# Four layers on one core: first images loaded ahead of the constants, one image held in a big tile, and new due times for the order of work

## The chip, the core and the metric

The kernel runs on one core of a Trainium2 chip. The core has five engines that run side by side: TensorE (PE, matrix products; its weight loads are listed apart as PEld), VectorE (DVE), ScalarE (ACT), GpSimd (POOL) and SyncE (SP), which here only issues DMA transfers. GpSimd issues some transfers too. All of them wait for each other through semaphores, and each engine executes its own instructions strictly in the order in which they stand in its program. The metric is the device time of one execution in microseconds (us); lower is better.

## The reference

The input is 16 images of 96 channels and 56 x 56 pixels (L = 3136). Four layers follow each other.

```
# layer 0: masked inverted bottleneck, 96 -> 576 -> 96
h = relu(bn(conv1x1(x, w_pw1))) * mask_dilate * vector
h = relu(bn(dwconv3x3(h))) * mask * vector
x = x + bn(conv1x1(h, w_pw2)) * mask

# layer 1: a four-direction selective scan (VMamba style) and an MLP
u = silu(dwconv3x3(layernorm(z) @ in_proj))          # 192 channels
dt, B, C = split(einsum(xs, x_proj))                 # four scan directions
dt = softplus(dt @ dt_proj + bias); a = exp(dt * A)
h[l] = a[l] * h[l-1] + dt * B * xs; y = h * C + D * xs
z = z + layernorm(sum of the four y) @ out_proj
z = z + gelu(layernorm(z) @ fc1) @ fc2; x = x + z

# layers 2 and 3, each: a Fourier filter and a quantized MLP
t = t + bn(ifft(relu(complex_scale(fft(relu(bn(ln(t) @ w1)))))) @ w2)
t = t + ffn(ln(t))      # inputs of the products rounded to fp8, sums to fp16
```

## The kernel before

The three functions `layer0`, `layer1` and `layers23` run one after the other, each with its own pools of on-chip memory. Layer 0 leaves its images in x1, layer 1 leaves its in x2, both in device memory. A layer can only start its loads once the memory that its tiles take over from the layer before is free.

**The order of the work.** Within a layer the instructions are not issued in source order. Each piece of work is a Python generator; before a group of instructions it yields an `Op` that names an engine, a guessed cost, buffers that it takes and gives back, and lists that it waits for. `in_order` (from line 277) keeps a clock for each engine and at each step picks, of all waiting pieces, the one with the smallest start plus `late`: `late(us, op)` (line 271) shifts the rank of one operation by a due time. A negative value lets it go ahead of others, a positive one lets others go ahead of it. Once picked, the instructions are recorded, so the order on every engine, on SP's DMA queue too, is fixed before the chip runs. The guessed costs decide nothing else, except one thing: `filling` (lines 348 to 358) puts filler products of the identity with itself on PE (line 354), in a number that follows from how long the planner sees PE idle:

```
for _ in range(min(int((idle[0] - 0.4) / 0.23), 32)):
    nc.tensor.matmul(p[:, :P], ident, ident, start=True, stop=True)
```

They fill the PE's idle time, and their results are overwritten. What stands in a layer's prologue (loads of constants, folding of weights) is recorded before `in_order` runs.

**Layer 1.** Per image there are these pieces. `front` loads the image in four pieces of up to 896 columns into "xc" (two buffers), squares each half on ACT into "xn" (one buffer, L761), sums both on PE (p_s, L767 and L768), copies the sums on DVE (L770) and takes the power -1/2 on GpSimd (L779). Then it loads the four pieces once more, spreads r over the channels by PE transposes (p_r, L789), multiplies on DVE into "xn" (L794), projects (p_in, L799), convolves by nine products per tap set (p_c, L840), applies SiLU, and makes the scan's inputs (p_x, L882), which go to device memory as bc (L895). `made_of` makes dt (p_d, L923, softplus L925) and a (exponential, L934), and loads the rows of bc as "rb" and "rc" (two buffers each, L945 and L949). `driven` multiplies dt on DVE by u (L978) and by rb (L982); `scanned` scans (L1002, L1004), multiplies by rc (L1009), adds into y (L1016, L1021), and at an image's end folds the two halves of ym (L1024). `back` does the rest for each group of 448 pixels: squares (L1049), p_o (L1056 to L1059), the power, p_y (L1079), z (L1082, L1084), sums and power again, p_t, p_f, GELU (L1117), p_g, and the store (L1128). The pieces of different images overlap. Seven big tiles of 128 x 3136 are handed around ("big"); the last of them also holds the raw constants during the prologue.

**Layers 2 and 3.** Four lanes hold one image each in a tile t. A lane is set to zero once by GpSimd (L1581, inside `lane`), then for each image t is loaded in two halves through SP (L1587), its mean and squares are reduced on DVE (L1318, L1313) and ACT (L1310), r is a power on GpSimd (L1330), and transposes (p_t, L1348), the projection p_a (L1358), and the short Fourier product (L1372) write to device memory (d, L1383), from where z is read back transposed (z<-d) for the next product (L1399). The lanes start 40 us apart in the planner's time.

Of the kernel before, what the change touches and what calls it, by code (L numbers as in the profile page):

```python
# [39 lines left out]
F32 = mybir.dt.float32  # L40
# [8 lines left out]
L = S * S  # L49
# [557 lines left out]
def layer1(ctx, tc, src, given, dst):  # L607
# [19 lines left out]

    ident = ph.c([P, P], "ident")
# [7 lines left out]
    big = [ph.c([P, L], f"big{i}") for i in range(buffers["big"])]  # L636
# [94 lines left out]
    def front(b, it):  # L731

        def loaded(g):
            n = min(896, L - 896 * g)
            x = buf([C, 896], "xc")[:, :n]
            nc.sync.dma_start(x, given[b][:, 896 * g : 896 * g + n])
            return x


        yield Op("POOL", 0.5, take=("x",))  # L740
# [5 lines left out]
        yield late(-1.0, Op("POOL", 0.7, take=("half",)))  # L746
# [8 lines left out]
        def sums(g):  # L755
            yield Op("SP", 0.3, 4.0, take=("xc",))
            x = loaded(g)
            for i in range(x.shape[1] // T):
                yield late(-0.2, act(T, take=("xn",)))
                sq = buf([C, 2, T], "xn")[:, 0]  # L760
                nc.scalar.activation(sq, x[:, T * i : T * i + T], AF.Square)  # L761
                last = i == x.shape[1] // T - 1
                yield late(0.2, pe(8, 0.193, give=("xn", "xc") if last else ("xn",)))
# [10 lines left out]
        yield late(-23.8, dve(0, over=0.4))  # L774
# [3 lines left out]
        yield late(1.6, Op("POOL", 6.5))  # L778
        nc.gpsimd.tensor_tensor(r, v, nhalf, ALU.pow)  # L779

        def projected(g):
            banks = 2 if g < 3 else 1
            yield late(0.2, Op("SP", 0.3, 4.0, take=("xc",)))
            x = loaded(g)
            yield late(-0.6, pe(4 * banks, 0.096, ("ps", "xn")))
# [6 lines left out]
            yield dve(448 * banks, give=("ps", "xc"))  # L792
            xn = buf([C, 2, T], "xn")[:, :banks]
            nc.vector.tensor_tensor(xn, x.rearrange("c (b n) -> c b n", n=T), p[:C, :banks, :T], ALU.mult)  # L794
            for j in range(2):
                yield pe(banks, 0.75, ("ps",), ("xn",) if j else ())
# [13 lines left out]
                for i, (low, row, n) in enumerate(parts):  # L810
# [3 lines left out]
                    yield act(S * n, over=0.15, give=("ps",) if i == len(parts) - 1 else ())  # L814
# [6 lines left out]
        yield [projected(g) for g in range(4)]  # L821
        it["u"] = us = []
        for j in range(2):
            yield late(0.4, Op("none", 0.0, 0.0, take=("big",)))
            us.append(big.pop(0))

        def convolved(j):

            pad, u = (whole, halves)[j], us[j]
            for c in range(0, (8, 4)[j], 2):  # L830
                yield Op("none", 0.0, 0.0, take=("ps",))
                p = pair("p_c")
                yield late(0.5, pe(9, 0.66, (), table="quarters"))
# [25 lines left out]
                for i, (out, in_, cost) in enumerate(outs):  # L859
                    yield late(0.4, act(cost, over=0.05, give=("ps",) if i == len(outs) - 1 else ()))  # L860
                    nc.scalar.copy(out, in_)
            yield late(-0.5, act(L, give=("x" if j == 0 else "half",), table="silu"))
# [7 lines left out]
        def inputs(g):  # L870
            yield late(1.0, pe(4, 1.42))
# [11 lines left out]
            yield late(-0.2, act(SUB, over=0.16, give=("ps",)))  # L883
# [7 lines left out]
        yield late(-52.7, Op("SP", 2.8, 4.0, post=it["ready"]))  # L891
# [13 lines left out]
    def made_of(it):  # L905
# [4 lines left out]
        def steps():  # L910

            for unit in units:
                i, h = unit
                order = (0, 1) if i < 3 else (1, 0)
                for s in order:
                    yield late(0.2, Op("none", 0.0, 0.0, take=("dt",)))
                    made[unit][s] = dt = buf([P, SUB], "dt")
                    yield late(-60.5, pe(1, 0.66, table="halves"))
# [5 lines left out]
                    yield late(-0.6, act(SUB, over=0.08, give=("ps",), table="softplus"))  # L924
# [4 lines left out]
                yield late(-39.2, Op("none", 0.0, 0.0, take=("a",)))  # L929
                made[unit]["a"] = a = buf([P, HALF], "a")  # L930
                for s in order:
                    give = ("proj",) if last and s == order[1] else ()
                    yield late(-0.6, act(SUB, over=0.18, give=give, table="exp", post=times[unit, s]))
                    nc.scalar.activation(a[:, SUB * s : SUB * s + SUB], made[unit][s], AF.Exp, scale=aneg[:, i : i + 1])  # L934

        def rows_of(k, tag):

            for unit in units:
                i, h = unit
                for s in halves_of(unit):  # L940
                    yield late(0.8, Op("SP", 0.2 if i in GROUP else 0.4, 4.0, take=(tag,), post=it[tag][unit, s]))
# [42 lines left out]
    def scanned(it):  # L984

        before, held = None, False
        for unit in units:
# [3 lines left out]
            if unit in ((0, 0), (2, 0)):  # L991
                yield Op("none", 0.0, 0.0, take=("big",))
                it["y"].append(big.pop(0))
            y = it["y"][mixed]
            for s in halves_of(unit):
                own, as_own, each = views(unit, s)
                yield late(-0.4, dve(SUB, 2.09e-3, wait=it["driven"][unit, s], give=("a",) if held else ()))
# [25 lines left out]
        yield late(-85.7, dve(L, 1.85e-3))  # L1023
        nc.vector.tensor_tensor(image(ym[:64]), image(ym[:64]), turned(ym[64:]), ALU.add)  # L1024

    def back(b, it):
# [4 lines left out]
        def group(g, own=None):  # L1031
# [15 lines left out]
            yield late(-0.3, act(T, take=tags("ysq")))  # L1047
            sq = new([P, 2, T], "ysq")
            nc.scalar.activation(sq[:, 0], y0[:, cols], AF.Square)  # L1049
            yield late(-28.8, act(T))  # L1050
# [15 lines left out]
            if it["left"] == 0:  # L1066
                big.extend((y0, ym))
                yield late(-11.7, Op("none", 0.0, 0.0, give=("big", "big")))
            small = lambda n: work.tile([Q, 4], F32, tag=n, name=n, bufs=8)
            v, r = small("v4"), small("r4")  # L1070
            yield late(-118.1, dve(0, over=0.33, give=("ps",)))
            nc.vector.scalar_tensor_tensor(v, o[:, :, C], -1.0, o[:, :, C], ALU.mult, ALU.mult)
            nc.vector.scalar_tensor_tensor(v, v, EPS, p[:Q, 4:, 0], ALU.add, ALU.add)
            yield Op("POOL", 1.85)
            nc.gpsimd.tensor_tensor(r, v, nhalf[:, :4], ALU.pow)
            yield late(-0.5, pe(4, 0.185, tags("ps", "z")))
# [6 lines left out]
            yield late(-31.0, dve(4 * C, give=("ps",)))  # L1083
# [3 lines left out]
            yield act(4 * C, take=tags("zn"))  # L1087
            zn = new([Q, 4, C], "zn")
            nc.scalar.activation(zn, z, AF.Square)
            yield late(-0.1, dve(4 * C))  # L1090
            nc.vector.tensor_reduce(s1, z, AX.X, ALU.add)
            yield late(-18.1, dve(4 * C, over=0.53))
# [4 lines left out]
            yield late(-45.2, Op("POOL", 1.85))  # L1097
# [3 lines left out]
            yield late(-19.7, pe(4, 0.085, tags("ps", "zt"), tags("zn")))  # L1101
# [3 lines left out]
            yield late(0.3, act(T, over=0.04, give=("ps",)))  # L1105
# [5 lines left out]
            yield late(-6.9, pe(3, 0.75, (), tags("zt")))  # L1111
# [3 lines left out]
            for j in range(3):  # L1115
                yield late(-0.7, act(T, over=0.16, table="gelu", give=("ps",) if j else (), lag=0.14 if j == 2 else 0.0))
                nc.scalar.activation(hid[:, j], ps[j // 2][:, j % 2, :T], AF.Gelu, bias=b_fc1[:, j : j + 1])  # L1117
            yield late(0.9, pe(16, 0.193, ("ps",), tags("hid", "xr")))
# [6 lines left out]
            yield dve(4 * C, give=("ps",))  # L1125
            nc.vector.tensor_tensor(z, z, p[:Q, :4, :C], ALU.add)
            yield late(-8.1, Op("SP", 0.3, 2.0))
# [34 lines left out]
    def makes():  # L1162
        for b in range(B):
            yield -1
            yield Op("none", 0.0, 0.0, wait=items[b]["ready"])
# [8 lines left out]
    def scans():  # L1174
        for b in range(B):
# [3 lines left out]
            yield late(2.0, Op("none", 0.0, 0.0, post=items[b]["done"]))  # L1179
# [457 lines left out]
```

## Time and profile before

| | us |
|---|---|
| Median of 3 runs (lowest, highest) | 7235.88 (7232.42, 7246.8) |
| The profiled execution | 7242.65 |
| Its span | 7240.9 |

| stretch of the span, us | what runs | PE busy | DVE busy | PE clock |
|---|---|---|---|---|
| 100 to 1640 | layer 0 | 1530.50 | 1493.40 | 1.00 |
| 1680 to 1720 | opening of layer 1 | 28.51 | 6.93 | 0.55 |
| 1760 to 1800 | first image's convolution | 39.76 | 0.00 | 1.00 |
| 2229 to 4480 | layer 1 in steady state | 2169.12 | 2081.45 | 0.99 |
| 4850 to 4890 | last groups of layer 1 | 28.38 | 3.87 | 0.92 |
| 4890 to 4950 | opening of layers 2 and 3 | 29.97 | 25.38 | 0.70 |
| 4950 to 5050 | their first transfers | 77.17 | 57.84 | 0.86 |
| 5600 to 7050 | layers 2 and 3 in steady state | 1378.82 | 1259.11 | 0.98 |

How to read the profile: a row of the windows view gives a stretch, its length, then the busy time of each engine with the number of instructions in brackets, the clock granted to PE as a share of full speed, the busy share of the 16 DMA engines, and what they moved in GB/s. A row of the groups view gives line, engine, operation, output<-inputs with shapes and count, then busy time and mean of one in ns, and, behind the last bar, the idle time of the engine just before these instructions with what ended it. A row of the timeline gives start, length, engine, line and, in square brackets, the idle time before it and its releaser. A matrix product of fp32 data shows as two records. The busy time of PE contains the fillers.

### The profile page before, as it was taken

What the parts mean: (1) busy time and instruction counts of PE and PEld (TensorE: products, weight loads), DVE (VectorE), ACT (ScalarE), POOL (GpSimd) and SP (SyncE); (2) the same over time, 40 slices, a digit from 0 to 9 for tenths busy, and PEclk for the clock granted to TensorE, in tenths of its full rate; (3) what the DMA queues carried; (4) which work ended last, traced back from release to release, by engine and by line L of the source; (5) the groups of instructions that cost most, each with busy time, mean ns of one, the idle gap of its engine ahead of it and who ended that gap; (6) DMA issues with size and microseconds to landing.
All of it is one profiled execution on the core that took longest, in us unless ns stands there. A gap on an engine that the chain in (4) does not pass through costs nothing.

```text
span 7240.9 us, 139640 instructions
## 1 busy us (share of the span) xinstructions
PE 6845.1 (95%) x57794; PEld 4734.2 (65%) x57794; DVE 6329.1 (87%) x8036; ACT 4814.4 (66%) x6165; POOL 1050.8 (15%) x804
## 2 busy tenths in 40 slices
PE   7999999999999999999999999986999999999998
PEld 3444444445666666666666666666887887887887
DVE  8999999992899999999999999965888898898897
ACT  4454544442677777777777777744777777777776
POOL 1000000000021222122222222121111111111111
PEclk9999999998999999999999999998999999999999
DMA  1100010001544444444444444426556656656653
GB/s 36 27 26 26 19 28 24 22 13 28 141 129 129 129 129 130 122 130 132 131 129 130 128 132 133 119 79 136 133 122 152 133 125 139 145 129 142 141 120 89
DMA packets 550245, 743.44 MB, mean 103 GB/s; under 512 B 258281, under 2 KB 388873, under 8 KB 546729
## 3 DMA queue, kind: packets, MB, share of 16 engines
q1 hardware_dynamic: 548425, 731.41, 40.3%
q8 instruction: 455, 7.45, 0.4%
q0 software_dynamic: 1184, 3.10, 0.2%
q14 instruction: 181, 1.48, 0.1%
HBM read 542.35 MB, written 191.99 MB: 101 GB/s over the span
## 4 chain that ended last, share of the span: by engine, by line
PE 39%; DVE 14%; ACT 10%; issue 4%; DMA 4%; SPq 1%; POOL 0%; ACTq 0%; DVEq 0%; POOLq 0%
PE p_c L840 6%; PE p L1399 4%; PE p_a L1358 4%; ACT y L1541 3%; PE p_x L882 2%; PE p_g L1123 2%; PE p_d L923 2%; PE p_g L1554 2%; PE p_v L1440 2%; PE p_v L1441 2%; PE p_u L1451 2%; PE p L1372 2%; DVE dt L1009 2%; DMA xc<-x 2%; DVE dt L982 2%
## 5 line engine op out<-in xcount | busy, mean ns | idle before, releaser
L558 DVE SCALAR_TENSOR_TENSOR h<-pad,l_dw,h 128x1568 f32<-128x1568 f32 x704 | 1260.8, 1843 | 2.5
L530 PE MATMUL p_c<-pad,taps 64*64 64x392 f32 x8064 | 685.6, 490 | 1.5 <-ACT h L546 0.8
L1330 POOL TENSOR_TENSOR r<-v,nhalf 120x16 f32<-120x16 f32 (+1 forms) x128 | 364.0, 2911 | 1913.2 <-DVE v L1328 1487.0
L978 DVE TENSOR_TENSOR dt<-dt,big 128x784 f32<-128x784 f32 x384 | 457.0, 1190 | 116.3 <-ACT a L934 114.0
L530 PEld LDWEIGHTS p_c<-pad,taps 64*64 64x64 f32 x8064 | 302.0, 132 | 363.5 <-issue 355.5
L546 ACT ACTIVATE h<-p_c,shift 128x392 f32<-128x392 f32 x336 | 226.4, 674 | 396.3 <-PE p_c L530 393.0
L925 ACT ACTIVATE dt<-p_d 128x784 f32<-128x784 f32 x384 | 315.6, 822 | 236.4 <-PE p_d L923 233.4
L503 PE MATMUL p<-x,l_w 96*128 96x448 f32 (+3 forms) x1280 | 428.3, 512 | 6.0 <-DVE y L595 3.2
L1399 PE MATMUL p<-k_f,z 112*128 112x112 f32 x3072 | 388.6, 286 | 26.3 <-DMA z<-d 20.4
L1399 PEld LDWEIGHTS p<-k_f,z 112*128 112x128 f32 x3072 | 371.6, 200 | 59.4 <-ACT y L1541 31.9
L509 ACT ACTIVATE pad<-p,bn_t,bn_s 128x896 f32<-128x896 f32 (+2 forms) x432 | 322.4, 800 | 122.8 <-PE p L503 120.5
L840 PE MATMUL p_c<-x,taps 64*64 64x392 f32 x4608 | 394.2, 491 | 0.0
L1440 PE MATMUL p_v<-w,gg 128*112 128x97 f32 x2048 | 374.4, 265 | 6.0 <-ACT o L1559 4.7
L982 DVE TENSOR_TENSOR dt<-dt,rb 128x784 f32<-128x784 f32 x384 | 371.0, 966 | 3.2 <-DMA rb<-bc 2.1
L1441 PE MATMUL p_v<-w2both,gg 128*112 128x97 f32 x2048 | 373.1, 264 | 0.0
L1009 DVE TENSOR_TENSOR dt<-a,rc 128x784 f32<-128x784 f32 x384 | 371.9, 969 | 0.7
L580 PE MATMUL p<-h,l_w 128*96 128x392 f32 x1024 | 362.1, 496 | 1.3 <-ACT h L561 0.9
L923 PE MATMUL p_d<-proj,l_dt 64*128 64x392 f32 x1536 | 363.0, 550 | 0.0
L934 ACT ACTIVATE a<-dt,aneg 128x784 f32<-128x784 f32 x384 | 343.4, 941 | 17.1 <-DVE a L1004 14.9
L1004 DVE TENSOR_TENSOR_SCAN a<-a,dt 128x784 f32<-128x784 f32 x192 | 351.5, 1831 | 1.1
L1002 DVE TENSOR_TENSOR_SCAN a<-a,dt 128x784 f32<-128x784 f32 x192 | 351.1, 1829 | 0.5
L503 PEld LDWEIGHTS p<-x,l_w 96*128 96x128 f32 (+1 forms) x1280 | 208.0, 180 | 217.2 <-issue 177.0
(336 smaller groups left out, 16966.9 us busy)
## 6 DMA issues: line engine op xcount, KB each, us to landing
rb<-bc SPq DMA_DIRECT2D x256, 392.0 KB
rc<-bc SPq DMA_DIRECT2D x256, 392.0 KB
d<-v SPq DMA_DIRECT2D x448, 192.0 KB
z<-d SPq DMA_DIRECT2D x128, 672.0 KB
rb<-bc SPq DMA_DIRECT2D x256, 196.0 KB
rc<-bc SPq DMA_DIRECT2D x256, 196.0 KB
d<-v SPq DMA_DIRECT2D x256, 169.8 KB
v<-d SPq DMA_DIRECT2D x192, 194.0 KB
```

What stands on the lines that cost most here:

```text
L503: nc.tensor.matmul(p[n * i : n * i + n, t, :size], w1[:, P * j : P * j + n], images[b]["x"][:, cols], start=True, stop=True,)
L530: nc.tensor.matmul(p[to : to + 64, t, :TC], taps[64 * s : 64 * s + 64, j, i], pad[64 * s : 64 * s + 64, r0 : r0 + 7, i % 3 : i % 3 + S], s ...
L558: nc.vector.scalar_tensor_tensor(out, view, dw[:, j, i : i + 1], out, ALU.mult, ALU.add)
L840: nc.tensor.matmul(p[to : to + 64, b, :TC], taps[64 * s : 64 * s + 64, j, k], pad[64 * s : 64 * s + 64, r0 : r0 + 7, k % 3 : k % 3 + S], s ...
L923: nc.tensor.matmul(p[:, b, :TC], wdt[on, i], proj[on, at : at + TC], start=True, stop=True)
L978: nc.vector.tensor_tensor(as_own(dt), as_own(dt), own(u), ALU.mult)
L982: nc.vector.tensor_tensor(dt, dt, made["rb", s], ALU.mult)
L1009: nc.vector.tensor_tensor(dt, a, made["rc", s], ALU.mult)
L1330: nc.gpsimd.tensor_tensor(r, v, nhalf[:, :n], ALU.pow)
L1399: nc.tensor.matmul(p[:, q, :Q], flat[:, P * (3 * q + k) : P * (3 * q + k) + P], f2, start=True, stop=True)
L1440: nc.tensor.matmul(out, gs[2 * h][:, at + k], w["w2"][:, 2 * h], start=True, stop=False)
L1441: nc.tensor.matmul(out, gs[1][:, at + k], w["w2both"][:, h], start=False, stop=True)
```

## The change

It has three parts; nothing of what is computed changes.

1. In layer 1 the first image is loaded ahead of the constants, half through SP and half through GpSimd's queue, into a big tile. `front` treats image 0 apart (`held`): it reads the image from this tile in both passes, and puts the squares and later the normalized pieces into a second big tile, so that neither "xc" nor "xn" is taken. Both tiles are given back after the projection.
2. In layers 2 and 3 the four tiles t are allocated and zeroed ahead of everything else, two on GpSimd and two on DVE, and the first two images are loaded ahead of the constants. The lanes no longer zero their tile, and do not load the first two images.
3. The due times (`late`) of some hundred yields in layers 1 to 3 are other numbers; some are dropped, some are new. Costs, buffers and instructions stay as they were.

```diff
@@ layer1
+    big = [ph.c([P, L], f"big{i}") for i in range(buffers["big"])]
+    for k, engine in enumerate((nc.sync, nc.gpsimd)):
+        cols = slice(L // 2 * k, L // 2 * k + L // 2)
+        engine.dma_start(big[0][:C, cols], given[0][:, cols])
     ident = ph.c([P, P], "ident")
...
-    big = [ph.c([P, L], f"big{i}") for i in range(buffers["big"])]
     stage, used = big[-1], 0
...
+        held = b == 0
+        tags = (lambda *t: ()) if held else lambda *t: t
+        yield late(-10.2, Op("none", 0.0, 0.0, take=("big", "big") if held else ()))
+        if held:
+            image_, mixed = big.pop(0), big.pop(0)
+
         def loaded(g):
             n = min(896, L - 896 * g)
+            if held:
+                return image_[:C, 896 * g : 896 * g + n]
...
-            yield Op("SP", 0.3, 4.0, take=("xc",))
+            yield late(-12.6, Op("SP", 0.0 if held else 0.3, 0.0 if held else 4.0, take=tags("xc")))
...
-                yield late(-0.2, act(T, take=("xn",)))
-                sq = buf([C, 2, T], "xn")[:, 0]
+                yield late(0.2, act(T, take=tags("xn")))
+                at = 896 * g + T * i
+                sq = mixed[:C, at : at + T] if held else buf([C, 2, T], "xn")[:, 0]
...
-            xn = buf([C, 2, T], "xn")[:, :banks]
+            if held:
+                xn = mixed[:C, 896 * g : 896 * g + T * banks].rearrange("c (b n) -> c b n", n=T)
+            else:
+                xn = buf([C, 2, T], "xn")[:, :banks]
...
         yield [projected(g) for g in range(4)]
+        yield Op("none", 0.0, 0.0, give=("big", "big") if held else ())
+        if held:
+            big.extend((image_, mixed))
...
-            yield late(1.0, pe(4, 1.42))
+            yield late(0.7, pe(4, 1.42))
             p = pair("p_x")
...
-                    yield late(0.2, Op("none", 0.0, 0.0, take=("dt",)))
+                    yield late(-36.2, Op("none", 0.0, 0.0, take=("dt",)))
                     made[unit][s] = dt = buf([P, SUB], "dt")
-                    yield late(-60.5, pe(1, 0.66, table="halves"))
+                    yield late(-161.2, pe(1, 0.66, table="halves"))
                     p = pair("p_d")
...
-                yield late(-39.2, Op("none", 0.0, 0.0, take=("a",)))
+                yield late(2.1, Op("none", 0.0, 0.0, take=("a",)))
...
-                    yield late(0.8, Op("SP", 0.2 if i in GROUP else 0.4, 4.0, take=(tag,), post=it[tag][unit, s]))
+                    yield late(0.5, Op("SP", 0.2 if i in GROUP else 0.4, 4.0, take=(tag,), post=it[tag][unit, s]))
...
-        yield late(-85.7, dve(L, 1.85e-3))
+        yield late(-0.1, dve(L, 1.85e-3))
...
-            yield late(-0.5, pe(4, 0.185, tags("ps", "z")))
+            yield late(-99.5, pe(4, 0.185, tags("ps", "z")))
             p = pair("p_y", P)
@@ layers23
     C1 = C + 1
+    lanes = [ts.tile([ROWS_Q, M, C1], F32, tag="t", name="t") for _ in range(LANES)]
+
+    def fetch(t, b, engines):
+        for j, engine in enumerate(engines):
+            engine.dma_start(t[64 * j : 64 * j + S, :, :C], given[b].rearrange("(n j m) c -> j n m c", j=2, m=M)[j])
+
+    for i, t in enumerate(lanes):
+        (nc.gpsimd, nc.vector)[i % 2].memset(t, 0.0)
+        if i < 2:
+            fetch(t, i, (nc.sync, nc.gpsimd))
+
...
-            yield late(-73.5, pe(16, 0.193, ("ps", "v"), give))
+            yield late(1.1, pe(16, 0.193, ("ps", "v"), give))
             own = vs.pop(0)
             p = pair("p_v")
...
-    def lane(images, wait):
+    def lane(t, images, wait):
         yield Op("none", 0.0, wait)
-        t = ts.tile([ROWS_Q, M, C1], F32, tag="t", name="t")
-        yield Op("POOL", 8.0)
-        nc.gpsimd.memset(t, 0.0)
         while images:
             b = images.pop(0)
             yield b
-            yield late(-1.2, Op("SP", 0.3, 8.0))
-            for j in range(2):
-                nc.sync.dma_start(
-                    t[64 * j : 64 * j + S, :, :C], given[b].rearrange("(n j m) c -> j n m c", j=2, m=M)[j]
-                )
+            there = b < 2 and t is lanes[b]
+            yield Op("SP", 0.3, 0.0 if there else 8.0)
+            if not there:
+                fetch(t, b, (nc.sync, nc.sync))
...
-        in_order(buffers, [lane(images, 40.0 * i) for i in range(LANES)], idle)
+        in_order(buffers, [lane(t, images, 40.0 * i) for i, t in enumerate(lanes)], idle)
```

## The prediction

> **What bounds the kernel now.** I read the page first, then the same numbers cut at the two layer borders, then the waits inside one stage. The page's busy line and its slices:
>
> ```profile
> PE 6845.1 (95%) x57794; PEld 4734.2 (65%) x57794; DVE 6329.1 (87%) x8036; ACT 4814.4 (66%) x6165; POOL 1050.8 (15%) x804
> ...
> PE   7999999999999999999999999986999999999998
> ...
> DVE  8999999992899999999999999965888898898897
> ```
>
> TensorE and VectorE are both full nearly everywhere. The holes are in the tenth slice (layer 0 to layer 1, near 1700 us) and the 27th and 28th (end of layer 1, start of layers 2 and 3, 4790 to 4970 us). The busy times by stretch (PE, PEld, DVE, ACT, POOL, then clock, DMA share, GB/s):
>
> ```profile
> 2229.00:4480.00 2251.00, 2169.12 (x17126) 1450.48 (x17119) 2081.45 (x2521) 1756.53 (x2230) 464.14 (x359) 0.99 0.47 129
> 5050.00:7050.00 2000.00, 1900.16 (x20063) 1653.14 (x20061) 1730.40 (x2737) 1460.45 (x1966) 325.09 (x116) 0.98 0.61 136
> 1680.00:1690.00 10.00, 0.87 (x6) 0.80 (x6) 1.79 (x13) 1.92 (x3) 6.15 (x19) 0.50 0.73 193
> ...
> 1700.00:1710.00 10.00, 10.00 (x55) 10.00 (x53) 0.42 (x3) 1.15 (x2) 0.00 (x0) 0.50 0.01 2
> 1710.00:1720.00 10.00, 9.94 (x69) 9.78 (x69) 0.52 (x3) 1.73 (x3) 0.00 (x0) 0.72 0.18 52
> 4880.00:4890.00 10.00, 0.00 (x0) 0.00 (x0) 0.55 (x5) 0.00 (x0) 5.97 (x12) 0.66 0.92 240
> 4890.00:4900.00 10.00, 0.00 (x0) 0.00 (x0) 3.35 (x23) 0.00 (x0) 2.46 (x5) 0.50 0.94 205
> ```
>
> The first row is nearly twelve images of layer 1 in steady state. The chain of waits has the same products of p_c begin at 2223.4 and, twelve images on, at 4487.5: 188.7 us per image, of which by the row's shares DVE is busy 174.5 and PE 181.8. But PE's figure contains fillers (L354, a product of the identity with itself, put in where the planner sees PE idle). A filler is two records; 64 records take 7.34 us at 1723 us, so one filler is 0.23 us. An image has 59 of them, 13.6 us, so PE's own work is 168.2 us and VectorE is the fuller engine, with 14.2 us of stalls per image. What ends them (last column):
>
> ```profile
> L978 DVE TENSOR_TENSOR dt<-dt,big 128x784 f32<-128x784 f32 x286 | 340.5, 1190 | 30.9 <-ACT a L934 29.0
> ...
> L1084 DVE TENSOR_TENSOR z<-z,p_y 112x384 f32<-112x384 f32 x84 | 46.5, 554 | 48.7 <-PE p_y L1079 41.7 <-DVE z L1082 0.5
> ...
> L770 DVE COPY me<-p_s 112x8 f32<-112x8 f32 x84 | 13.3, 158 | 30.1 <-PE p_s L768 30.0
> ```
>
> Over 12 images: 3.5 us per image for p_y, 2.5 for p_s, 2.4 for the exponential. These are stalls of order: the data come from an engine that did something else first. So time can come from a better order and from the two borders.
>
> **Part 1: layer 1's opening.** Before, each square (ACT) waits until PE has read the square before it, because "xn" has one buffer:
>
> ```profile
> 1702.53 0.58 ACT L761 ACTIVATE xn<-xc 96x448 f32<-96x448 f32 x1 [12.37 <-PE p_s L768]
> 1706.40 0.58 ACT L761 ACTIVATE xn<-xc 96x448 f32<-96x448 f32 x1 [3.30 <-PE p_s L768]
> ```
>
> The seven groups of p_s run from 1699.3 to 1723.4, 24.1 us. With all squares in a big tile, PE goes through them without a stop. A group took 3.2 us of PE at clock 0.50 and 1.84 at full clock. Here a rule and the row differ. "TensorE: Matmul & The Clock Gate" (What's actually happening) has the clock released after about 3.4 us of sustained work: one cold group and six warm, 3.2 + 11.0 = 14.2 us, a gain of 9.9. The rows show PE busy 10.00 of 10 us at clock 0.50, and 0.72 in the next ten: some 15 us of these small matmuls before the release. By the row: five cold, two warm, 19.7 us, a gain of 4.4. I take the row. The projection behind it ran from 1730.3 to 1752.0, 21.7 us, with one "xn" shared by four groups; in the listing of the order in which the new program's instructions stand on each engine, all 28 transposes (3.2 us) stand ahead of the 14 matmuls of 0.84 us (11.7), and the first needs one 1.1 us product on DVE: 16.5 us, a gain of 5.2.
>
> Against it: the image (1.204 MB) is now ahead of the 18 constants on both queues. "DMA: Bandwidth & Descriptors" (Issuing engines are not separate DMA queues) says that queues of different issuers share the same 16 engines, so the second queue buys issue time and no bandwidth: the constants wait. At the row's 193 GB/s the image takes 6.2 us; two loads of xc (0.69 MB) that shared that stretch go, 3.6 us; the last constants come 2.6 us later. Did each issuer have bandwidth of its own, this would be 0. PE's first products wait for k_c at 1691.0, so I charge 2.6. Sum: 4.4 + 5.2 - 2.6 = **7 us** (ends -2 and +12).
>
> **Part 2: the opening of layers 2 and 3.** From the timeline:
>
> ```profile
> 4909.08 1.75 DVE L1318 TENSOR_REDUCE mean<-t 120x16 f32<-120x1536 f32 x1
> ...
> 4919.19 3.52 PE L1348 MATMUL p_t<-ident,t 120*97 120x120 f32 x16 [11.49 <-DVE t L1341]
> ...
> 4944.49 1.82 SPq L1587 DMA_DIRECT2D t<-x  x2
> ...
> 4966.34 6.50 PE L1399 MATMUL p<-k_f,z 112*128 112x112 f32 x32 [20.38 <-DMA z<-d]
> ```
>
> DVE folds constants until 4909.1, then reduces the first image (7.2 us), then GpSimd's power, then PE starts at 4919.2. In the new order the reductions and the power stand ahead of the folding, in the wait for constants, so PE can start some 10 us earlier. The second image and the missing half of the first (1.8 MB at 240 GB/s, 7.5 us) are ahead of the constants, though in the listing one half on SP stands ahead of layer 1's last two stores and the two on GpSimd's queue behind none, some 3 to 5 us earlier than the 4880.9 of before; of the folding, 5 us hang on the last constants. I take 9 us gained (2 to 14). Later, the second image's load, 1.2 MB, sat at 4944.5 just ahead of the z<-d transfers that PE awaits; it goes, worth 5.6 us at 215 GB/s; I take 6 (0 to 9). The wait itself stays: the new order still has the first image's p behind 32 fillers and z<-d. The zeroing of t on GpSimd (2.4 us each) moves into the border, partly onto DVE, which idles there from 4881.9 to 4892.8: nothing. Sum: **15 us** (2 to 23).
>
> **Part 3: the new due times.** These move instructions, and the trace cannot show that order. What the listing shows is a count: fillers fall from 1740 to 1263. Per repeating image of layer 1 (13 of them) 59 become 39: 20 x 0.23 = 4.6 us. Images 2 and 3 lose 19 together, 4.4 us. In layers 2 and 3 a round of four images goes from 50 to 3 (10.8 us), three rounds and the last four images lose 150, 34.5 us. All in all 59.8 + 4.4 + 34.5 = 98.7 us of idle that the new order fills with work. That is not yet time: a filler taken out where PE still has to wait only becomes idle. What speaks for real gain is where things went. p_y, which stood behind 12 matmuls of p_x and two of p_d, no longer does; the p_d products come early, so the exponential is ahead of DVE; ACT's table loads fall from 540 to 522. Below stands nothing (all becomes idle), above everything plus the rest of DVE's waits. DVE's named waits were 10.1 us per image, over twice the 4.6, so there is room; PE's records show 6.9 us per image of idle beyond the fillers, so the chip does not follow the plan to the end. I take three quarters, **74 us**.
>
> **Sum.** 7 + 15 + 74 = 96 us. The profiled execution took 7242.65 (span 7240.9 and 1.75 around it): 7146.7. It was 6.8 us above the median of the runs, 7235.88; on that I forecast **7140 us**, 1.3% faster.
>
> **Rivals.**
> - *The order is worth nothing, only the borders count*: 7236 - 22 = 7214. For it: of DVE's 142 us of named waits in that stretch 70 end on ACT and GpSimd, whose work hardly changes. Against it: p_y alone is 3.5 us per image.
> - *All DVE waits on PE and ACT go*: 10.1 us x 15 images, 151, with 34 and 22: 7029. Against it: p_s stays behind the xc load.
> - *Slower: SP's queue.* The new order often issues two rb loads in a row with rc behind them: seven places in a repeating image, none before. "rb" has two buffers, so the second waits until DVE's L982 frees one, SP stands still, and rc, whose landing took 2.7 us in the chain of waits, comes late to L1009, which now waits 0.4 us in 286. At 1.5 us a place, about half a landing: 10.5 per image, 5.9 more than is gained, x15 = 88; less 22 and 26: 7276. It decides from 0.66 us a place (4.6/7). Against it: DVE's order has moved the same way, with two L982 ahead of an L1009.
> - *It doesn't do what it says*: the first image's loads do vanish from SP's listing, so no.
>
> **How the numbers follow.** Forecast 62%, own range 7095 to 7190; borders alone 18%; all waits gone 8%; slower 12%. Two runs can be told apart by about 0.2%, 14.5 us. Faster takes the forecast, the 8% and five sixths of the second: 0.85. Same: 0.05. Slower: 0.10. The range runs from 7070 (inside the third case) to 7225 (past the second).
>
> **What would show it.** Right: layer 1 repeats every 184 to 186 us, L1084's wait on p_y nearly gone, L1009's still below 1 us in all; the seven p_s groups in about 20 us; PE at work in layers 2 and 3 some 9 us sooner after layer 1's last store; rounds of four images some 8 us below the 563 and 567 between their loads of t now. Wrong: an unchanged period with more PE idle, or DVE waits on rb and rc of tens of microseconds.

## The result and the profile after

| | us | against before |
|---|---|---|
| Before, median of 5 runs (lowest, highest) | 7239.89 (7232.42, 7248.42) | |
| After, median of 5 runs (lowest, highest) | 7201.4 (7190.5, 7216.83) | 0.9947, 95% interval 0.993 to 0.9964 |
| After, profiled execution and its span | 7201.4, 7199.6 | |

The change is 38 us (0.5%) faster. I forecast 96 us. The page after, busy times and the slices of PE and DVE:

```profile
PE 6782.9 (94%) x56840; PEld 4639.8 (64%) x56840; DVE 6352.1 (88%) x8038; ACT 4807.8 (67%) x6147; POOL 1004.4 (14%) x805
...
PE   7999999999999999999999999978999999999998
...
DVE  8999999992999999999999999966888888888887
```

PE's 27th and 28th slices went from 8 and 6 to 7 and 8, and the last twelve of DVE hold no 9 any more. So I cut both traces at the same events: the end of layer 0 on DVE (L598), the first product of p_c, the issue of layer 1's last store, the first short Fourier product behind z<-d (L1399 before, L1429 after), and the end.

| stretch | before, us | after, us | gain | forecast |
|---|---|---|---|---|
| end of layer 0 | at 1677.5 | at 1674.7 | 2.8 (the program there is the same) | 0 |
| to the end of the first projection, then p_c | 74.1 | 65.8 | 8 | 7 |
| layer 1 up to its last store | to 4879.0 | to 4799.6 | 68.6 | 48 (three quarters of 64.2) |
| last store to the first Fourier product | 87.3 | 73.4 | 13.9 | 15 |
| from there to the end | 2274.5 | 2326.6 | **-52.1** | +26 (three quarters of 34.5) |

They sum to 41 us, the difference of the two profiled executions. Three of the four forecast steps came near the forecast or above it. The last one has the wrong sign: 78 us off, more than the missing 58. These are the windows of after, twelve images of layer 1 first, then the last stretch, then the seven groups of p_s:

```profile
2199.81:4410.75 2210.94, 2137.14 (x16752) 1395.39 (x16752) 2108.42 (x2533) 1764.22 (x2232) 444.58 (x360) 0.99 0.48 133
4873.00:7199.60 2326.60, 2138.09 (x22248) 1844.77 (x22248) 1920.59 (x3039) 1639.50 (x2193) 335.95 (x124) 0.96 0.59 129
1697.00:1707.00 10.00, 10.00 (x54) 9.67 (x53) 1.07 (x4) 0.00 (x0) 0.00 (x0) 0.50 0.01 2
1707.00:1717.00 10.00, 10.00 (x55) 10.00 (x55) 0.52 (x3) 0.00 (x0) 0.00 (x0) 0.50 0.00 0
1717.00:1727.00 10.00, 10.00 (x70) 10.00 (x69) 0.59 (x3) 0.00 (x0) 4.82 (x1) 0.73 0.01 2
```

Twelve images take 2210.94 us, 184.2 each (before 188.7), and DVE is now busy 95% of it (before 92.5%). What ended DVE's idle time there:

```profile
L997 DVE TENSOR_TENSOR dt<-dt,big 128x784 f32<-128x784 f32 x289 | 343.2, 1188 | 9.1 <-ACT a L953 8.0
...
L1028 DVE TENSOR_TENSOR dt<-a,rc 128x784 f32<-128x784 f32 x288 | 279.6, 971 | 3.1 <-issue 0.2
L1001 DVE TENSOR_TENSOR dt<-dt,rb 128x784 f32<-128x784 f32 x288 | 278.8, 968 | 15.4 <-DMA rb<-bc 14.2
...
L1103 DVE TENSOR_TENSOR z<-z,p_y 112x384 f32<-112x384 f32 x84 | 46.6, 554 | 8.8
...
L783 DVE COPY me<-p_s 112x8 f32<-112x8 f32 x84 | 13.7, 163 | 1.5 <-PE p_s L781 1.5
```

The waits for p_y (41.7 us in twelve images) are gone, those for p_s fell from 30.0 to 1.5, those for the exponential from 29.0 to 8.0. New is the wait for rb, 14.2 us, 1.2 per image: SP's queue is felt, but at a quarter of the 4.6 us per image from which it would have decided.

The last stretch of before, to be laid beside that of after:

```profile
4966.30:7240.90 2274.60, 2141.59 (x22594) 1864.45 (x22594) 1921.44 (x3038) 1636.10 (x2193) 359.32 (x127) 0.98 0.59 132
```

It holds three full rounds of four images. After, they took 577, 570 and 568 us (5390 to 7105), where I had expected 8 below the 563 and 567 of before. PE's records fell by 346, which is 173 fillers or 40 us of work. Yet PE's busy time hardly fell (2141.59 to 2138.09): the granted clock went from 0.98 to 0.96. The record of the clock in these traces knows only 1.00 and 0.50; PE spends 169 us of this stretch at 0.50 ("half clock" from here on), before 104.

**Where the holes come from.** The view of one line, ScalarE's copy of p into a tile of v (L1409), with what its engine waited for and who waited for it (us, times):

```profile
  DMA d<-v: 80.7, 35
  PE p L1402: 42.7, 51
...
  PE p_f L1568: 42.4, 22
```

Before, the same view of its twin L1379:

```profile
  PE p L1372: 92.4, 55
  DMA d<-v: 2.8, 3
```

The tiles of v form a ring of nine: each is filled, stored to d, and reused. The new order comes round to a tile before its store has landed. ScalarE stands still, and with it the PSUM tile, which holds PE's product, that it is to empty, for which PE's p_f waits. One such place in ScalarE's and PE's timelines:

```profile
5455.58 2.20 ACT L1409 COPY v<-p 128x768 f32<-128x768 f32 x3 [3.42 <-DMA d<-v]
...
5456.43 0.90 PE L1568 MATMUL p_f<-xq,fw1q 96*128 96x480 fp8e5 x2 [2.68 <-ACT v L1409]
```

And the windows around it:

```profile
5445.00:5453.00 8.00, 6.78 (x100) 5.42 (x98) 7.93 (x13) 5.11 (x9) 0.00 (x0) 1.00 0.84 135
5453.00:5457.00 4.00, 1.32 (x12) 0.31 (x4) 3.48 (x4) 1.42 (x3) 0.00 (x0) 0.94 0.55 150
5457.00:5463.50 6.50, 6.50 (x21) 5.54 (x21) 1.82 (x2) 3.50 (x7) 0.00 (x0) 0.51 0.63 183
5463.50:5470.00 6.50, 6.42 (x107) 4.96 (x106) 5.60 (x11) 6.50 (x9) 0.00 (x0) 1.00 0.24 60
```

A wait of 3.42 us on ScalarE becomes a hole of 2.68 us on PE, and behind it PE works 6.5 us at half clock. It pays twice. In three rounds PE has 11 holes of over 2 us where before had none; 8 of the 11 end on this copy.

### The profile page after: what moved, and what is told of

The parts are those of the page before. It is cut to its first block, busy times and chain, and to the rows that moved or that the text cites. A ratio compares the mean times of both kernels' runs of the same rounds, so it can differ in the third digit from the quotient of the medians.

```text
span 7199.6 us, 137700 instructions
## 1 busy us (share of the span) xinstructions
PE 6782.9 (94%) x56840; PEld 4639.8 (64%) x56840; DVE 6352.1 (88%) x8038; ACT 4807.8 (67%) x6147; POOL 1004.4 (14%) x805
## 3 DMA queue, kind: packets, MB, share of 16 engines
q1 hardware_dynamic: 544477, 728.39, 40.6%
## 4 chain that ended last, share of the span: by engine, by line
PE 59%; DVE 21%; ACT 9%; issue 5%; DMA 5%; SPq 1%; POOL 0%; DVEq 0%; ACTq 0%; POOLq 0%
PE p_c L859 8%; PE p_c L530 7%; DVE h L558 4%; PE p L503 4%; PE p L580 4%; PE p_a L1388 3%; PE p_v L1470 3%; PE p_v L1471 3%; PE p_x L901 3%; PE p_f L1133 3%; PE p_d L942 2%; PE p_u L1481 2%; PE p_g L1142 2%; ACT y L1571 2%; PE p_g L1584 2%
## 5 line engine op out<-in xcount | busy, mean ns | idle before, releaser
L1360 POOL TENSOR_TENSOR r<-v,nhalf 120x12 f32<-120x12 f32 (+1 forms) x128 | 346.3, 2726 | 1992.8 <-DVE v L1358 1992.7
L1429 PE MATMUL p<-k_f,z 112*128 112x112 f32 x3072 | 360.4, 278 | 21.9 <-DMA z<-d 14.9
L1429 PEld LDWEIGHTS p<-k_f,z 112*128 112x128 f32 x3072 | 355.0, 194 | 31.1 <-issue 16.2
L1388 PE MATMUL p_a<-first,xt 97*120 97x192 f32 x1792 | 353.4, 357 | 21.5 <-DVE v L1391 11.2
L1117 POOL TENSOR_TENSOR r<-v,nhalf 112x4 f32<-112x4 f32 x112 | 234.3, 2092 | 850.7 <-DVE v L1115 849.8
```

The costliest lines, as they stand in the source:

```text
L1388: nc.tensor.matmul(p[:ROWS_Q, j, :HW], xt[:, at + j], w["first"], start=True, stop=True)
L1429: nc.tensor.matmul(p[:, q, :Q], flat[:, P * (3 * q + k) : P * (3 * q + k) + P], f2, start=True, stop=True)
```

## The experiments

All ratios are to the kernel before, measured with each set of runs.

| run | median, us | ratio (95%) |
|---|---|---|
| layer 1 alone changed | 7165.71 | 0.9895 (0.9879 to 0.991) |
| layers 2 and 3 alone changed | 7257.77 | 1.0027 (1.0019 to 1.0035) |
| after, ten tiles in v | 7144.82 | 0.9866 (0.9852 to 0.9879) |
| after, old due times in layers 2 and 3 | 7294.53 | 1.0073 (1.006 to 1.0086) |
| the same with the old plan kept | 7157.03 | 0.988 (0.9868 to 0.9893) |
| ten tiles, no fillers in layers 1 to 3 | 7192.38 | 0.993 (0.9918 to 0.9943) |
| after, store of o first | 7201.3 | 0.9944 (0.9922 to 0.9966) |
| ten tiles, p_y's due time undone | 7253.87 | 1.0014 (1.0005 to 1.0022) |
| ten tiles, no fillers in layers 2 and 3 | 7150.65 | 0.9872 (0.9859 to 0.9886) |
| old plan, no fillers in layers 2 and 3 | 7142.98 | 0.9861 (0.9846 to 0.9876) |
| before, first image held, nothing else | 7243.93 | 0.9997 (0.9988 to 1.0005) |
| ten tiles and store of o first | 7151.38 | 0.9882 (0.9865 to 0.9898) |

**1 and 2: each half alone.** The functions `layer1` and `layers23` of the two kernels, exchanged:

```diff
 layer1    # of after
-layers23  # of after
+layers23  # of before
```

> Layer 1 as in the changed kernel (held first image, new due times), layers 2 and 3 as before. Theory: the whole gain lies in layer 1 and layers 2 and 3 gave part of it back. In the two traces layer 1's last store is issued 79.4 us earlier (4879.0 to 4799.7), and layers 2 and 3 took 2361.9 us from there before, 2399.9 after. So 4799.7 + 2361.9 + 1.8 = 7163 us, 38 below the changed kernel. Rival: the layers borrow from each other (what is early at layer 1's end is only waited for later), then about 7200 as the changed kernel.

> Layer 1 as before, layers 2 and 3 as in the changed kernel (early loads of t and new due times). Theory (layers 2 and 3 lose 38 us net, 14 gained at their opening and 52 lost behind it): 4879.0 + 2399.9 + 1.8 = 7281 us. Rival (they gain as forecast, 15 + 26, and the loss comes only from meeting the new layer 1): 7200.

Layer 1 alone gives 7165.71 us, as its theory said (7163), and beats the whole change: 0.9895 and 0.9947 have separate intervals. Layers 2 and 3 alone, at 7257.77 us, lie between the two theories (7281 and 7200) and are slower than before, so their loss does not come only from meeting the new layer 1. Its size is not the same everywhere: 19 us beside the old layer 1, 36 beside the new one. From the last store on, the traces have 2381.4 us in the second run and 2399.9 in the changed kernel, with 127 and 169 us of the last stretch at half clock. ScalarE's waits for tiles of v are much the same in both, 74 and 81 us. I did not find out what makes the clock differ between executions of one order.

**3: a tenth tile in the ring.** Only the ring grows; the planner still counts nine. The room comes from w2, of which only two of three parts are kept.

```diff
-    vs = [ph.c([P, 8 * C1], f"v{i}") for i in range(buffers["v"])]
+    vs = [ph.c([P, 8 * C1], f"v{i}") for i in range(buffers["v"] + 1)]
...
-        w2 = ph.c([P, 3, C1], f"w2_{i}")
+        w2 = spare[:, 3 * C1 * i : 3 * C1 * i + 3 * C1].rearrange("p (k c) -> p k c", k=3)
...
-        w["w2"] = w2
+        w["w2"] = ph.c([P, 2, C1], f"w2_{i}")
+        nc.vector.tensor_copy(w["w2"], w2[:, 0:3:2])
```

> The changed kernel with ten tiles in the ring v instead of nine; the planner still counts nine, so every engine's order behind the prologue stays as it is. In layers 2 and 3 ScalarE's copy of p into v (L1409) waits 80.7 us for a store of d to release its tile (before 1.9 in three rounds of four images), and PE's p_f waits 42 us for the PSUM tile that this copy holds. Theory V (that wait is the cause of the loss): it falls below 15 us, PE's time at half clock falls with it, and the time falls by 30 to 50 us: 7150 to 7172. Theory C (the clock: 173 fillers fewer, so PE is gated more often whatever the holes are made of) and theory O (the order itself, ScalarE doing other pieces first): the wait goes, but the time falls by less than 12 us: 7190 to 7200.

It took 7144.82 us, 57 less than the changed kernel. Its rounds took 561, 557 and 556 us. The whole last stretch:

```profile
4874.10:7148.90 2274.80, 2103.19 (x22248) 1820.33 (x22248) 1918.66 (x3039) 1637.81 (x2193) 334.57 (x124) 0.98 0.59 132
```

This row is to be laid beside that of after: the same 22248 records, but PE needs 2103.19 us for them instead of 2138.09. That is 35 us of clock. The rest of the 52 us is idle time (188.5 to 171.6, 17 us). At half clock PE spends 104 us again, and of the holes of over 2 us in three rounds 3 are left of 11. In layers 2 and 3 other runs have the same order on PE, DVE and ScalarE (in 7 and 12 SP's order differs by the stores of o), and their traces agree:

| order of layers 2 and 3, tiles in v | last stretch, us | of it at half clock, us |
|---|---|---|
| old, nine (before, experiments 1 and 5) | 2274.5, 2278.6, 2272.4 | 104, 108, 105 |
| new, nine (after, experiments 2 and 7) | 2326.6, 2301.8, 2331.7 | 169, 127, 174 |
| new, ten (experiments 3, 8 and 12) | 2274.9, 2270.3, 2264.5 | 104, 103, 94 |

So the number of tiles is what costs the new order its loss, and C and O fall: there are no more fillers than in the changed kernel, and the order is the same. (The room for the tile comes from w2. No run moves w2 alone, so its part in this is not separated.)

Theory V had one number wrong: ScalarE's wait did not fall below 15 us.

```profile
  DMA d<-v: 50.5, 28
  PE p L1404: 44.8, 54
...
  PEld p_a L1390: 44.7, 22
  PE p_a L1390: 34.5, 22
```

It is at 50.5 and now holds up p_a, and a second copy (L1476) now waits 16.6 us for its tile: 67.1 us in all copies, after 81.3. The tenth tile did not take the wait away; it moved and shortened it, so that fewer holes on PE are long. That the shorter holes are what gave the clock back is read from the traces; no run varied the holes alone.

**4 and 5: the early loads with the old order.**

Against `layers23` of before, with the tiles and the two loads put ahead of the constants as in the change, the fourth kernel has `lane` as in the change, three due times of its own included:

```diff
-        yield Op("POOL", 8.0)
-        nc.gpsimd.memset(t, 0.0)
...
-            yield late(-1.2, Op("SP", 0.3, 8.0))
+            yield Op("SP", 0.3, 0.0 if there else 8.0)
...
-            yield late(-6.1, Op("none", 0.0, 2.0))
+            yield Op("none", 0.0, 2.0)
...
-            yield late(0.8, Op("none", 0.0, 0.0, take=("z",)))
+            yield Op("none", 0.0, 0.0, take=("z",))
```

The fifth only leaves out the instructions, and tells the planner nothing:

```diff
         yield Op("POOL", 8.0)
-        nc.gpsimd.memset(t, 0.0)
...
             yield late(-1.2, Op("SP", 0.3, 8.0))
-            for j in range(2):
...
+            if not (b < 2 and t is lanes[b]):
+                fetch(t, b, (nc.sync, nc.sync))
```

> The changed kernel with the due times of layers 2 and 3 as before, but their tiles t and first two images early. The planner now puts 612 fillers into these layers instead of 307 with the old opening and 134 with the new due times. If fillers tell of time (my forecast's reading, 0.23 us each): 70 us slower than layer 1 alone changed, less 14 for the opening: about 7219. If the fillers are no measure and the chip's own waits decide: 14 us faster than layer 1 alone changed, about 7149.

> Layer 1 alone changed, and in layers 2 and 3 the tiles t and the first two images early, while the planner is told of the same operations as before, so that the order behind the prologue stays the old one (307 fillers). Theory: the 129 us that the early loads with old due times lost against layer 1 alone come from the planner's answer to the shorter opening, not from the loads. Then the opening's gain stands alone: 7166 less 7 to 14 us (first L1429 or its twin comes 73 us after layer 1's last store instead of 80 to 87): 7152 to 7159. Rival: the early loads themselves cost (they hold up layer 1's last store by 6.6 us and bring the lanes together): 7166 or more.

The fourth is 129 us slower than layer 1 alone changed, which neither of its forecasts had. The fifth is 9 us faster, as its theory said (7152 to 7159), though the difference of the ratios, 0.0015, is inside their intervals. Both load early. In the fourth the planner was told, put everything in another order, and saw 612 fillers' worth of idle PE. Its last stretch:

```profile
4861.70:7280.60 2418.90, 2241.75 (x23204) 1958.35 (x23204) 1923.96 (x3039) 1637.20 (x2193) 339.38 (x124) 0.96 0.56 124
```

It is 144 us longer than in experiment 3. Here due times are worth something only in the plan for which they were found: two cheaper operations and three other numbers in `lane` cost 137 us against the fifth.

**6, 9, 10: fillers.** In each, one function is emptied, in the layers named in the table:

```diff
-    fill = filling(nc, idle, ident)
+    fill = lambda p: None
```

> The kernel with ten tiles in v, but no fillers in layers 1 to 3 (1229 products of the identity left out; nothing that is computed changes). Theory I (a filler stands in idle time and is worth nothing): 7145 within 10 us, time at half clock as it was (about 85 us in layer 1, 104 in layers 2 and 3). Theory K (the fillers hold the clock up): layer 1's holes of up to 32 fillers, 7 us, become idle, the clock falls to 0.5 behind each; at three such spells of 3.4 to 6.8 us per image 130 to 250 us more at half clock, so 65 to 125 us slower: 7210 to 7270.

> The kernel with ten tiles in v, without fillers in layers 2 and 3 alone (134 products of the identity left out; nothing that is computed changes). In the kernel without any fillers in layers 1 to 3 the part from the first L1429 on took 2261.7 us against 2274.9, its opening 71.3 against 73.2. If that was the fillers' own time, 15 us less: 7130. If it was chance, or borrowed from a layer 1 that ended later: 7145 within 5.

> Layer 1 as changed, early loads with the old plan in layers 2 and 3, and no fillers there (307 products of the identity left out). Theory I (a filler there stands in a hole that stays, and no hole is long enough to cost clock): 7157 within 8 us. Theory H (a filler there is time, 0.23 us each): up to 63 us less, 7094. Theory K (the fillers hold the clock, as in layer 1): time at half clock rises from 105 us, and the time by 15 us or more: over 7172.

The sixth took 7192.38 us, 48 above its base: neither theory holds for the whole. Layer 1 of its base (experiment 3), then layer 1 and the last stretch without fillers:

```profile
1741.00:4800.90 3059.90, 2938.46 (x23122) 1956.86 (x23120) 2814.80 (x3365) 2331.79 (x2955) 588.39 (x475) 0.99 0.44 127
...
1741.00:4867.90 3126.90, 2830.20 (x20923) 1798.47 (x20921) 2818.48 (x3365) 2329.82 (x2953) 586.04 (x475) 0.93 0.43 124
4939.20:7200.90 2261.70, 2082.98 (x22044) 1800.06 (x22044) 1918.91 (x3039) 1637.08 (x2193) 335.27 (x124) 0.97 0.59 133
```

In layer 1 the clock falls to 0.93 (454 us at half clock, 85 with fillers), and the layer ends 67 us later: there the fillers hold the clock. In layers 2 and 3 no time is lost. The 13 us that this trace seems to gain there did not come again: with the fillers left out there alone the time is 7150.65, its ratio inside the interval of ten tiles with fillers. The tenth shows it in the old order. Its last stretch, first with fillers (experiment 5), then without:

```profile
4872.80:7145.30 2272.50, 2141.63 (x22594) 1864.26 (x22594) 1921.37 (x3038) 1636.80 (x2193) 354.90 (x124) 0.98 0.59 132
...
4871.70:7144.60 2272.90, 2096.39 (x22044) 1813.56 (x22044) 1921.39 (x3038) 1636.34 (x2193) 354.80 (x124) 0.97 0.59 132
```

PE is busy 45 us less and stands idle for 46 more. The clock is not the same, though: without fillers half clock takes 140 us of this stretch instead of 105, as theory K said, and in the ninth 132 instead of 104. So the fillers hold some clock here too, but the time does not follow: at 0.9861 against 0.988 the tenth is no slower, and faster by no more than the intervals allow.

**7 and 12: the store of o.** In the changed kernel the stores of o (L1490) go out 1.24 us behind their copies on average and 9.88 at most (before 0.06 and 1.37; the 1.40 in the expectation was counted in three rounds), since SP stands at a load of z ahead of them.

```diff
-            yield late(3.0, Op("SP", 0.7, 2.0))
+            yield Op("SP", 0.7, 2.0)
             for ri in range(2):
```

> The changed kernel with nine tiles in v, one due time undone: the store of o (L1490) has 0 instead of +3.0 on SP. The planner's fillers stay 134. In the trace this store is issued 1.40 us behind its copy on average, 6.19 at the ninth tenth and 9.88 at most (before 0.03 and 0.69 at most), because SP stands at a load of z that waits for stores of d; its tile of v comes back so much later. Theory S (SP's order makes the tiles late): ScalarE's waits for d<-v fall from 80.7 us to under 50 and the time by 20 to 55 us: 7146 to 7181. Theory N (nine tiles are too few for this order however the stores stand): less than 15 us, 7186 or more.

> Both edits of the ring together: ten tiles in v, and the store of o at 0 instead of +3.0 on SP. With ten tiles alone ScalarE still waits 50.5 us for d<-v and the time was 7145; with the store alone the waits stayed at 77.6 of 80.7 and the time at 7201. If, with a tile to spare, the late stores are what is left of the wait: it falls below 25 us, and the time by 10 to 25 us, to 7120 to 7135. If not: 7145 within 8 us, with the wait at 40 to 50.

The delay fell to 0.57 us, but ScalarE's wait only from 80.7 to 77.6, and the time not at all (7201.3). With ten tiles as well the wait is at 44.8 and the time at 7151.38; its interval overlaps that of ten tiles alone. Theory S, which was mine, falls: the late stores of o are there, and they are not what empties the ring.

**8: p_y's due time.**

```diff
-            yield late(-99.5, pe(4, 0.185, tags("ps", "z")))
+            yield late(-0.5, pe(4, 0.185, tags("ps", "z")))
             p = pair("p_y", P)
```

> The kernel with ten tiles in v, with one due time of layer 1 undone: p_y at -0.5 instead of -99.5. The planner then puts 1510 fillers into layer 1 instead of 1095. Theory P (p_y's place is the heart of layer 1's gain): DVE waits for p_y again (before 3.5 us per image, 14 images): 7145 + 50 = 7195. Theory F (planned fillers are time in layer 1, 415 x 0.23 us): 7240. Theory W (the chip does not follow the plan, other due times carry the gain): 7145 to 7165.

It took 7253.87 us, 109 more than its base, and is the only single due time that I undid in layer 1. Theory F is nearest (95 us). The groups of DVE in layer 1 (2230 to 4480 us):

```profile
L997 DVE TENSOR_TENSOR dt<-dt,big 128x784 f32<-128x784 f32 x280 | 332.7, 1188 | 31.9 <-ACT a L953 31.3
...
L1103 DVE TENSOR_TENSOR z<-z,p_y 112x384 f32<-112x384 f32 x81 | 44.9, 554 | 37.2 <-PE p_y L1098 29.6
...
L783 DVE COPY me<-p_s 112x8 f32<-112x8 f32 x81 | 12.8, 162 | 25.6 <-PE p_s L781 25.3
...
L1091 DVE SCALAR_TENSOR_TENSOR v<-o 112x4 f32<-112x4 f32 x81 | 12.8, 157 | 46.5 <-ACT o L1083 46.1
```

The wait for p_y is back with 29.6 us, but so are those for p_s, the exponential and o (1.5, 8.0 and 5.5 us in the changed kernel's twelve images), whose due times were left alone. One number in the plan moved the order of much else.

**11: the held image alone.** The first image early in a big tile and its squares in another, in the kernel before, with the planner told of nothing:

```diff
+        held = b == 0
+        if held:
+            image_, mixed = big.pop(0), big.pop(0)
...
-                sq = buf([C, 2, T], "xn")[:, 0]
+                sq = mixed[:C, at : at + T] if held else buf([C, 2, T], "xn")[:, 0]
```

> The kernel before with the first part of the change alone: layer 1's first image loaded ahead of the constants and held, its squares and normalized pieces in a second big tile, while the planner is told of the same operations as before and every due time is the old one. My step said 4.4 + 5.2 - 2.6 = 7 us; the first product of p_c came 10.8 us earlier in the changed kernel, of which layer 0 gave 1: 7230 to 7233. The 5.2 us of the projection rest on its transposes standing ahead of its matmuls, which the old plan does not do: without them 7236. Rival (the early image delays the constants by as much): 7238 or more.

7243.93 against 7243.95 us: nothing. The squares were done 33 us earlier (11.5 us behind layer 0's end instead of 44.2), but the groups of p_s took 24.7 us as before 24.1. In this plan 20 fillers stand between the groups, 1.1 us for each two at half clock, in PE's own queue: PE was never without work there. In the changed kernel these fillers are gone and the transposes of p_r stand ahead of the projection, so the gain of the first part there comes with the new plan; the held image alone does not bring it.

## Why the prediction was right or wrong

- **Part 1, 7 us: right in size, 8, by terms that were each off.** The p_s groups took 21.1 us (forecast 19.7, gain 3.0 instead of 4.4), because PE stayed at half clock through all seven, 3.0 us each; the clock rose only at 1722.3. I had five cold groups and two warm. The rule of 3.4 us that I had weighed against the row would have given 14.2; the row was nearer, and still too short. And what went from between the groups was fillers, not waits for squares (experiment 11). Projection: 13.4 us where I had 16.5, gain 7.8 instead of 5.2. My terms sum to 16.0; its matmuls took 10.7 us instead of 11.7, and DVE's product ran beside the transposes. The constants made p_s 1.0 us later instead of 2.6; that lies between the 2.6 of shared engines and the 0 of separate ones, and settles neither. A term that I did not have took 1.7: the 31 fillers that stand beside GpSimd's power took 9.0 us, the first 4 of them at half clock, where 32 had taken 7.3, and held up the transposes to 3 us behind the power's end. So 3.0 + 7.8 - 1.0 - 1.7 comes to 8.
- **Part 2, 15 us: right in size, 13.9, but half of it for another reason.** PE's p_t came 33.7 us behind layer 1's last store (before 40.2), 6.5 us sooner instead of 9. I put that down to the early loads and the reductions ahead of the folding. But p_t comes at 33.1 us with layer 1 alone changed and no early loads (experiment 1), and at 40.6 with the early loads behind the old layer 1 (experiment 2). So this term came with the new end of layer 1, which is luck; what in it does this is open. Three halves of the two images, 1.8 MB, were issued ahead of layer 1's last store, and the constants, which wait for that store to land, went out 9.6 us behind its issue where they took 2.8 before. The other term was right: the wait at z<-d fell from 20.38 to 12.61 us, and it is 20.0 us in experiment 1 and 12.1 in experiment 2, so it goes with the early loads.
- **Part 3 in layer 1, 48 us: right in kind, too small.** By my count 64.2 us of fillers went, and 68.6 us of time. The trace of this stretch has 259 fillers fewer (59.6 us at 0.23 each); PE is busy 49.9 us less and idle 18.7 us less. So the count came near, but not because a filler is time in itself: leaving them all out made the layer slower (experiment 6). What went with them were DVE's waits for p_y, p_s and the exponential. (I also wrote that DVE's named waits were 10.1 us per image: those on PE and ACT were; all of them were 11.9.)
- **Part 3 in layers 2 and 3, 26 us: wrong. This is the step that failed.** I priced the 34.5 us of fillers that go at three quarters, and took "all becomes idle", which is nothing, for the worst case; a new wait in the new order, with its price in clock, I put at nothing without asking the trace. Measured: -52.1. With the ring relieved, 173 fillers fewer became 39 us more idle PE (2274.6 less 2141.59 is 133.0 before, and 171.6 with ten tiles) and the stretch took 2274.9 us as before 2274.5, so the fillers that went were worth nothing there; experiment 10 finds the same for all fillers of the old order. With nine tiles the wait for a tile of v comes on top: 52 us in this trace, of which 35 are clock and 17 idle time; 27 to 57 us in the three traces of this order. What stays open: with ten tiles PE's p_a still waits 34.5 us for that copy, and no run has a ring so large that the wait is gone, so the new order might be worth something there.
- **Rivals.** The borders did give 22. SP's queue in layer 1 cost 1.2 us per image at rb, below what would have decided. What happened was a slower rival that I did not have: the new order of layers 2 and 3 against its ring. The view was there to be asked: before, all copies into v together waited 8.4 us for their stores (L1379 2.8). That told that nine tiles were enough for the old order, not how near they were to too few.

With ten tiles the time is 7144.82 us, close to the 7140 forecast, but by luck, not by my sum: layer 1 gave more, layers 2 and 3 nothing.

**The faster kernels.** Ten tiles in v (0.9866), and the new layer 1 with early loads under the old plan, with fillers (0.988) or without (0.9861): all beat before and the change, and the intervals do not tell these apart.

## What to carry to other kernels

A planner's idle time is not a price until the chip has confirmed it for that stage. In layer 1 it told the size (64 us planned, 69 measured; p_y undone, 95 and 109), in layers 2 and 3 it did not (40 planned, 0 measured with ten tiles; experiments 4 and 5, 305 fillers apart, 70 and 137). So ask for each stage what the plan does not know, above all when a buffer comes back from a transfer. When an order is changed, look at every ring, also one whose wait is near zero now. And look at the clock behind a hole on TensorE: in the changed kernel's trace twice as much was lost behind the holes as in them (35 us and 17). But test it, since in experiment 10 another 35 us at half clock cost nothing.

## What the runs showed of the hardware

- The granted clock changes on a fixed grid of 3.413 us. In layers 1 to 3 of before, after and the kernel with ten tiles, the clock fell behind 122 such windows; in none of them had PE been idle for less than 1.10 us. Of the windows at full clock with over 1.2 us of idle PE, it fell behind 111 and not behind 90; with over 1.92 us it always fell. The Trainium skill, "TensorE: Matmul & The Clock Gate" (What's actually happening), names one idle window of some 3.4 us as what throttles; here a third of one was enough, about half of the time. (A few per cent of PE's records can be missing, so the idle times are upper values.)
- Going up can take longer than one full window: PE was busy 10.00 of 10 us twice in a row at 0.50 at layer 1's opening. Of the 122 spells at half clock behind those windows, 104 lasted one or two windows of the grid.
- Fillers can hold the clock and be worth it (layer 1: 67 us), or hold it for nothing (layers 2 and 3 under the old plan: without 275 of them 35 us more at half clock, and 0.4 us more time), in one program.
